# GpSimd's edge columns ahead of the difference, small steps and table sums by VectorE, two of three images in the combined form

## The chip, the cores and the metric

One Trainium2 chip, one core. The time is the device time of one execution in microseconds (us), given as the median of three runs. The engines named here are TensorE (PE: matmuls; PEld: its weight loads), VectorE (DVE), ScalarE (ACT), GpSimd (POOL) and SyncE (SP, which issues the plain transfers). SBUF is the on-chip memory, PSUM the accumulators that TensorE writes.

## What is computed

An input `x` of 160 images, 128 channels, 32x32 pixels, is group-normalised (32 groups of 4 channels, per image) and convolved with a 3x3 kernel, and the result is added to `x`. There are five sets of weights; image number `b*5+n` of the input uses set `n`. The weights are quantised in two stages from `U`, with step sizes taken from the maximum and minimum of the whole of `U`.

```python
def _L0_conv_ref(x, U):
    beta = jnp.max(U); alpha = jnp.min(U)
    s1 = (beta - alpha) / 3.0
    v1 = s1 * floor(U / s1)
    s2 = s1 / 5.0
    v2 = s2 * floor((U - v1) / s2)
    w = (v1 + v2).reshape(OUT_CH * N, IN_CH, 3, 3)
    xb = x.reshape(B // N, N * C, H, W)
    act = conv_general_dilated(xb, w, (1, 1), padding 1, feature_group_count=N)
    return act.reshape(B, C, H, W)
def _gn(v, G=32, eps=1e-5):
    g = v.reshape(B, G, C // G, H, W)
    m = mean(g, (2, 3, 4)); s = var(g, (2, 3, 4))
    return ((g - m) / sqrt(s + eps)).reshape(v.shape)
x = x + _L0_conv_ref(_gn(x), U)
```

## The kernel before

The kernel works set by set, 32 images to a set, image `i` from 0 to 159. Channels lie on the 128 partitions, an image is 1024 float32 on each. Images come in chunks of two (tile `xt`, eleven chunks in the pool), and leave by chunks too.

**Precision.** The normalised image is split into a high and a low float16 part; the weights are small multiples of one step and exact in float16.

**Two forms of an image.** Each form saves multiplications by pairing neighbours (a sum and a difference of neighbouring rows or columns, multiplied with sums and differences of taps). The loop takes one of them per image, chosen by `combined(i)` (line 563):

- *not combined* (rows): `z` is the normalised image (GpSimd, line 625, or ScalarE, line 552, for an image that starts a group of statistics), `hi` its float16 part (ScalarE, 560), `lo` the rest (VectorE, 650), and three VectorE instructions build the pair sums `rows` from `lo` (663, 671, 672). TensorE does 18 matmuls on `hi` (687) and 12 on `rows` (742): 30.
- *combined* (columns): `v` holds differences and sums of neighbouring columns of the raw image. VectorE writes most of it (602, 609), GpSimd one quarter, the difference of odd and even columns (619), and the two edge columns (590). ScalarE makes the float16 `vh` from it (637), VectorE the rest `vl` (643). TensorE does 24 matmuls (742).

`combined(i)` is true, from image 7, for odd images up to 125, for three of five up to 145 and for two of three after that: 82 images.

**The loop.** In iteration `i` TensorE runs `conv(i)` (761): first `sums_of_pairs(i+1)`, six matmuls into the bank `m2` and six into `m1`, then the main products of image `i` into its own bank pair `eo`. Beside it, each on its own engine, in program order:

- VectorE: the low part of image `i+2` (`low_combined` or `low_part` and `combinations`), one or two instructions of the next set's weights (`take(later, ...)`, fourteen instructions for each of three columns of taps), `pairs(i+1)` (799, 801: reads `m1` in PSUM and `m2`, writes `eo`), `combine(i+4)` (602, 609).
- ScalarE: the first statistics pass of an image about 14 ahead (201), the copy `sum` of the finished image `i-1` out of PSUM (827), `leave(i+1)` (790: `m2` out of PSUM), `hi` or `vh` of image `i+3`, the second statistics pass (208).
- GpSimd: the quarter of `v` or the `z` of image `i+4` (`beside_pairs`; a dependency written by hand makes it wait for the last VectorE instruction ahead of `pairs`), the transfer that adds `sum` to the image in SBUF (850, `accumulate`), the small steps of the statistics, the sums of the weight tables, and last the edge columns (590).
- SP: the store of a finished chunk (855), then the next load (426).

**The residual.** Mostly ScalarE copies the result out of PSUM and a GpSimd transfer adds it to `xt`. Where `by_hand(i)` is true (the first three images, the last four, and every eighth from image 31) VectorE adds the result to the image itself (844) and there is no transfer.

**Small steps.** The images fall into groups (2, 2, 4, 4, 4, 4, 4, then 8 each). For each group TensorE averages over channels (216, 233), ScalarE copies the results (225, 239), and GpSimd does eight small instructions (227 to 230, 243, 247, 250, 252), among them the power -0.5 (243).

**Tables.** The weights of the next set are quantised by VectorE, turned by TensorE and copied by ScalarE (496). GpSimd then makes, for each column, the sum and the difference tables (502 to 504), and after the third column the same over columns (`across`). The order of all of this is written out by hand; each engine works its own queue in order.

Of the kernel before, what the change touches and what calls it, by code (L numbers as in the profile page):

```python
# [19 lines left out]
ROW = 3  # L20
# [146 lines left out]
class Statistics:  # L167
# [5 lines left out]
    def __init__(self, nc, small, gavg, mhalf, nb, scale, name):  # L173
        self.nc, self.small, self.gavg, self.mhalf = nc, small, gavg, mhalf
        self.nb, self.scale, self.name = nb, scale, name

        self.mv = self.tile("mv", [nb, 2])
# [57 lines left out]
    def deviation(self):  # L235

        nc = self.nc
        ve = self.tile("ve", [self.nb])
        nc.scalar.activation(
            ve, self.pg[:, 1, :], ACTF.Copy, scale=1.0 / self.size, bias=EPS  # L240
        )
        self.rstd = self.tile("rstd", [self.nb])
        nc.gpsimd.tensor_tensor(self.rstd, ve, self.mhalf[:, : self.nb], ALU.pow)  # L243
# [11 lines left out]
def general_path(tc, keep, steps, x, u, out):  # L255
# [8 lines left out]
    with tc.If(far > 0), ExitStack() as ctx:  # L264
# [9 lines left out]
        for n in range(N_SETS):  # L274
# [11 lines left out]
            with tc.For_i(0, IMGS // N_SETS, 1) as b:  # L286
# [7 lines left out]
                stats.deviation()  # L294
                stats.scales()
# [22 lines left out]
class Main:  # L318
# [28 lines left out]
    FIFTHS = 126  # L347
    THIRDS = 146
    EARLY = 8
    FIRST = 3  # L350

# [5 lines left out]
    def __init__(self, tc, ctx, keep, x, u, out):  # L357
# [42 lines left out]
        self.wts, self.across = {}, {}  # L400
# [91 lines left out]
    def keep_taps(self, n, col):  # L492

        P = self.P
        wt = self.wpool.tile([P, 5, P], MM, tag=f"wt{col}", name=f"wt{n}_{col}")
        self.nc.scalar.mul(wt[:, self.G, :], self.pt, 1.0 / LIFT)  # L496
        self.wts[n, col] = wt

    def both_sums(self, total, diff, g0, g1, g2):

        pool = self.nc.gpsimd
        pool.tensor_tensor(total, g0, g2, ALU.add)
        pool.tensor_tensor(diff, total, g1, ALU.subtract)
        pool.tensor_tensor(total, total, g1, ALU.add)

    def keep_sums(self, n, col):
        wt = self.wts[n, col]
        self.both_sums(wt[:, self.SUM], wt[:, self.DIFF], *(wt[:, k] for k in range(ROW)))
        if col == self.COLS[-1]:
            across = self.wpool.tile(  # L510
                [self.P, 2, ROW, self.P], MM, tag="across", name=f"across{n}"
            )
            self.across[n] = across
            self.both_sums(
                across[:, 0], across[:, 1], *(self.wts[n, c][:, self.G] for c in range(ROW))
            )
# [69 lines left out]
    def outer_columns(self, i):  # L586

        W, H = self.W, self.H
        st, j = self.column_of(i)
        self.nc.gpsimd.tensor_scalar(  # L590
            self.view(self.v[i], 0, (512 + W // 2 - 1, 2), (W // 2, H)),
            self.view(self.image(i), 1, (W - 3, 2), (W, H)),
            st.ngm[:, j], -1.0, ALU.add, ALU.mult,
        )
# [18 lines left out]
    def beside_pairs(self, i, after):  # L613

        nc = self.nc
        if self.combined(i):
            self.v[i] = self.wide.tile([self.P, 2048], F32, tag="v", name=f"v{i}")
            even, odd = (self.image(i)[:, a::2] for a in range(2))
            ins = nc.gpsimd.tensor_sub(self.v[i][:, 1536:], odd, even)  # L619
        elif self.by_scalar_too(i):  # L620
            return
        else:
            st, j = self.column_of(i)
            z = self.z[i] = self.zpool.tile([self.P, 1024], F32, tag="z", name=f"z{i}")
            ins = nc.gpsimd.tensor_scalar(  # L625
                z, self.image(i), st.ngm[:, j], st.rstd[:, j], ALU.add, ALU.mult
            )
        self.tc.add_manual_dep(
            ins.ins, after.ins.name,
# [229 lines left out]
    def run(self):  # L859
# [75 lines left out]
        self.stats[0].deviation()  # L935
        measure(1, 2)
# [9 lines left out]
        self.stats[1].deviation()  # L946
        self.stats[1].scales()
# [38 lines left out]
        ready, middle, measured, loaded = [], [], self.EARLY, 6  # L986
        later, turned = iter(()), []
        for i in range(self.imgs):
# [15 lines left out]
            if i < self.FIRST:  # L1004
# [6 lines left out]
                if i == 0:  # L1011
                    self.stats[2].variances()
                    self.stats[2].deviation()
                    self.stats[2].scales()
# [32 lines left out]
            else:  # L1047
# [8 lines left out]
                last = take(later, i % 2, last)  # L1056
# [12 lines left out]
                for st in ready:  # L1069
                    st.deviations()  # L1070
# [8 lines left out]
            for st in middle:  # L1079
                st.deviation()  # L1080
                st.scales()
# [79 lines left out]
```

## Time and profile before

| | |
|---|---|
| median of three runs (lowest, highest) | 1014.31 us (1011.05, 1015.3) |
| the profiled execution | 1012.46 us, span 1010.8 us |
| granted TensorE clock, mean over the span | 0.992 |
| combined images / others | 82 / 78 |
| images added by a transfer / by VectorE | 137 / 23 |
| span from the `pairs` of image 64 to those of image 96 | 434.39 to 627.50 us |
| the same, image 96 to 128 | 627.50 to 820.33 us |

The profile is one execution. Its page gives busy time per engine, waits by releaser, groups of instructions with their mean durations, and shares of the sixteen transfer engines. "Busy" counts the time in which at least one instruction of the engine is open, and instructions overlap by some 0.05 to 0.1 us, so the cost of one instruction in a full queue is read from start to start in the timeline, not from its duration. The starts of line 799, one for each image, give the pace of the loop.

### The profile page before, as it was taken

The numbers are of one execution on the slowest core, as the hardware profiler recorded it, in microseconds if no ns is written. First come the engines' busy times: TensorE is split into PE (matmuls) and PEld (weight loads), VectorE is DVE, ScalarE is ACT, GpSimd is POOL, SyncE is SP. The second block draws the span as 40 slices with busy tenths as digits, with TensorE's granted clock in tenths as the row PEclk, the third lists the DMA queues.
The fourth block names the chain that finished last, engine by engine and source line by source line (L and its number), as shares of the span: only waits on it lengthen the run. The fifth ranks groups of instructions, "written<-read, shape, count | busy, mean of one in ns | idle before, by whom it ended". The sixth has DMA issues, their size and how long they took to land.

```text
span 1010.8 us, 13191 instructions
## 1 busy us (share of the span) xinstructions
PE 951.7 (94%) x4504; PEld 441.5 (44%) x4504; DVE 899.1 (89%) x1175; ACT 831.5 (82%) x1154; POOL 575.2 (57%) x622
## 2 busy tenths in 40 slices
PE   2889999998999999989999999999999989999997
PEld 1434444444444444434444444444444434444443
DVE  7988999997998999788989897988999987979995
ACT  5768989898898988889889888897988978899551
POOL 4346575665646466655556565646465776456740
PEclk9999999999999999999999999999999989999999
DMA  9528899999997988988988989998989798997774
GB/s 360 196 89 232 219 271 257 267 254 254 270 307 185 306 224 266 246 258 236 258 243 242 260 264 245 280 258 257 242 250 285 206 255 212 276 250 208 182 201 157
DMA packets 65116, 245.85 MB, mean 243 GB/s; under 512 B 5008, under 2 KB 5008, under 8 KB 65040
## 3 DMA queue, kind: packets, MB, share of 16 engines
q1 hardware_dynamic: 45312, 173.09, 48.8%
q0 software_dynamic: 19728, 71.84, 37.1%
q8 instruction: 37, 0.61, 0.2%
q14 instruction: 39, 0.32, 0.1%
HBM read 89.19 MB, written 83.89 MB: 171 GB/s over the span
## 4 chain that ended last, share of the span: by engine, by line
ACT 25%; POOL 24%; PE 18%; DVE 16%; issue 15%; DMA 1%; POOLq 0%; DVEq 0%; ACTq 0%
ACT vh L637 7%; ACT junk L208 7%; PE eo L687 6%; PE eo L742 5%; POOL v L590 4%; ACT sum L827 4%; PE m L742 3%; POOL rstd L243 3%; POOL xt L850 3%; ACT m L790 3%; POOL v L619 2%; DVE lo L650 2%; DVE v L602 2%; DVE eo L799 2%; DVE eo L801 2%
## 5 line engine op out<-in xcount | busy, mean ns | idle before, releaser
L687 PE MATMUL eo<-hi,wt 128*128 128x496 f16 (+2 forms) x1386 | 369.3, 376 | 0.8 <-ACT wt L496 0.8
L742 PEld LDWEIGHTS <-wt 128*128 128x128 f16 x1884 | 184.1, 99 | 208.4 <-issue 0.9
L637 ACT ACTIVATE vh<-v,rstd 128x2048 f16<-128x2048 f32 x82 | 164.2, 2003 | 73.9 <-POOL v L590 73.5
L643 DVE SCALAR_TENSOR_TENSOR vl<-v,rstd,vh 128x2048 f16<-128x2048 f32 x82 | 193.0, 2354 | 33.1 <-ACT vh L637 32.5
L687 PEld LDWEIGHTS <-wt 128*128 128x128 f16 x1458 | 143.1, 99 | 165.9 <-issue 2.5
L619 POOL TENSOR_TENSOR v<-xt 128x512 f32<-128x512 f32 x82 | 85.7, 1045 | 209.1 <-DVE vl L643 52.9
L742 PE MATMUL eo<-vh,wt 128*128 128x496 f16 (+1 forms) x492 | 184.3, 375 | 0.0
L742 PE MATMUL eo<-vl,wt 128*128 128x496 f16 (+1 forms) x492 | 184.2, 374 | 0.0
L201 ACT ACTIVATE junk<-xt 128x1024 f16<-128x1024 f32 x152 | 160.6, 1057 | 19.2 <-DMA xt<-in_x_dram 15.7
L208 ACT ACTIVATE junk<-xt,mv 128x1024 f16<-128x1024 f32 x152 | 174.0, 1145 | 0.1
L742 PE MATMUL eo<-rows,wt 128*128 128x496 f16 (+1 forms) x450 | 171.4, 381 | 0.0
L742 PEld LDWEIGHTS <-across 128*128 128x128 f16 x984 | 97.0, 99 | 139.6 <-issue 27.7
L827 ACT COPY sum<-eo 128x1024 f32<-128x1024 f32 x137 | 141.9, 1036 | 15.9 <-PE eo L742 15.9
L590 POOL TENSOR_SCALAR v<-xt,ngm 128x64 f32<-128x64 f32 x82 | 120.4, 1469 | 59.5 <-DVE v L602 59.2
L850 POOL DMA_DIRECT2D xt<-sum x137 | 120.8, 881 | 2.8 <-issue 1.9
L790 ACT ACTIVATE m<-m 128x512 f32<-128x512 f32 x157 | 93.7, 597 | 26.7 <-PE m L742 20.6
L742 PE MATMUL m<-vh,across 128*128 128x496 f16 (+1 forms) x246 | 93.3, 379 | 21.2 <-ACT m L790 17.1
L625 POOL TENSOR_SCALAR z<-xt,ngm,rstd 128x1024 f32<-128x1024 f32 x53 | 62.9, 1187 | 64.5 <-DVE rows L672 55.5
L602 DVE TENSOR_TENSOR v<-xt 128x960 f32<-128x960 f32 x82 | 97.4, 1187 | 0.0
L650 DVE TENSOR_TENSOR lo<-z,hi 128x1024 f16<-128x1024 f32 x78 | 96.0, 1231 | 0.0
L742 PE MATMUL m<-vl,across 128*128 128x496 f16 (+1 forms) x246 | 93.5, 380 | 0.0
L799 DVE SCALAR_TENSOR_TENSOR eo<-m1a,m 128x512 f32<-128x512 f32 x78 | 54.3, 696 | 40.7 <-ACT m L790 36.8
(131 smaller groups left out, 1301.4 us busy)
## 6 DMA issues: line engine op xcount, KB each, us to landing
xt<-in_x_dram SPq DMA_DIRECT2D x78, 1024.0 KB, 9.6
out_dram<-xt SPq DMA_DIRECT2D x78, 1024.0 KB, 5.9
xt<-sum POOLq DMA_DIRECT2D x137, 512.0 KB, 6.2
u<-in_L_conv_U_dram SPq DMA_DIRECT2D x4, 576.0 KB, 10.9
xt<-in_x_dram SPq DMA_DIRECT2D x4, 512.0 KB, 9.7
range<-in_L_conv_U_dram SPq DMA_DIRECT2D x3, 576.0 KB, 7.9
out_dram<-xt SPq DMA_DIRECT2D x3, 512.0 KB, 2.7
u<-in_L_conv_U_dram SPq DMA_DIRECT2D x2, 288.0 KB, 3.1
```

What stands on the lines that cost most here:

```text
L201: self.nc.scalar.activation(junk, image, ACTF.Copy, scale=-1.0 / image.shape[1], accum_out=self.mv[:, j, 0:1],)
L208: self.nc.scalar.activation(junk, image, ACTF.Square, bias=self.mv[:, j, 0:1], accum_out=self.mv[:, j, 1:2],)
L590: self.nc.gpsimd.tensor_scalar(self.view(self.v[i], 0, (512 + W // 2 - 1, 2), (W // 2, H)), self.view(self.image(i), 1, (W - 3, 2), (W, H) ...
L602: nc.vector.tensor_tensor(self.view(v, 1, (511, 2), (half, H), (1, half - 1)), self.view(x, 1, (1, 2), (W, H), (2, half - 1)), self.view(x ...
L637: self.nc.scalar.mul(vh, self.v[i], st.rstd[:, j])
L643: yield self.nc.vector.scalar_tensor_tensor(vl, self.v[i], st.rstd[:, j], self.hi[i], ALU.mult, ALU.subtract)
L650: self.nc.vector.tensor_sub(lo[:, 1 : self.H + 1, :].rearrange("p h w -> p (h w)"), self.z.pop(i), self.hi[i].rearrange("p h w -> p (h w)"),)
L687: nc.tensor.matmul(self.bank(target, a)[:, first:end, c0:c1], self.wts[n, col][:, k, :], tile[:, s0 : s0 + 2 * (end - first) - 1 : 2, c0 + ...
L742: self.nc.tensor.matmul(out, weights, moving, start=start and j == 0, stop=False, skip_group_check=True)
L790: self.nc.scalar.mul(m2, self.m2_ps, 0.5)
L827: nc.scalar.copy(self.as_banks(i, self.sum[i]), self.flat(i, eo))
L850: self.nc.gpsimd.dma_start(self.image(i), self.sum.pop(i), accum_op=ALU.add)
```

## The change

- `combined(i)` is `i % 3 != 1` from image 7 on: 102 images are combined, 58 are not. A group can now begin with a combined image, which needs no `z` by ScalarE.
- `by_hand(i)` holds for the first three and the last four images only.
- The edge columns (`outer_columns`) move from the end of GpSimd's work of an iteration to `beside_pairs`, ahead of the quarter of differences, and both get the dependency on the last VectorE instruction ahead of `pairs`. VectorE's `combine` of the same image comes after them.
- For all groups but those that start at images 0, 2, 4, 8 and 24 (`late`), VectorE does five small steps straight from PSUM (`deviations_by_vector`) and two more (`scales_by_vector`); GpSimd keeps the power, which runs one iteration later than before, ahead of `beside_pairs`. ScalarE no longer copies the means for them.
- The three column tables of a set are one tile. For sets 1 to 4 VectorE makes the sums: three instructions for the three columns at once and three for `across`, taken one or two at a time from `later` after the third column.
- `take(later, ...)` takes two instructions with a combined image and one otherwise (before: one with odd images, none with even ones); the instruction taken with `low_part` and the one taken where there is no `combine` stay.

```diff
@@ Statistics
         nc.scalar.activation(
             ve, self.pg[:, 1, :], ACTF.Copy, scale=1.0 / self.size, bias=EPS
         )
-        self.rstd = self.tile("rstd", [self.nb])
-        nc.gpsimd.tensor_tensor(self.rstd, ve, self.mhalf[:, : self.nb], ALU.pow)
+        self.ve = ve
+
+    def power(self):
+        self.rstd = self.tile("rstd", [self.nb])
+        return self.nc.gpsimd.tensor_tensor(
+            self.rstd, self.ve, self.mhalf[:, : self.nb], ALU.pow
+        )
+
+    def deviations_by_vector(self):
...
+        means = self.pg[:, 0, :]
+        vector.tensor_scalar_mul(self.twice, means, 2.0)
+        vector.tensor_tensor(self.dv, mv[:, :, 0], means, ALU.subtract)
+        vector.tensor_copy(self.ngm, means)
+        vector.scalar_tensor_tensor(
+            self.dv, self.dv, float(self.size), self.dv, ALU.mult, ALU.mult
+        )
+        vector.tensor_add(self.dv, self.dv, mv[:, :, 1])
+
+    def scales_by_vector(self):
...
+        vector.tensor_scalar_mul(self.rstd, self.rstd, self.scale)
+        self.shift = self.tile("shift", [self.nb])
+        vector.tensor_tensor(self.shift, self.ngm, self.rstd, ALU.mult)
@@ Main
+    HURRIED = (0, 2, 4, 8, 24)
...
+    def sums_of_set(self, n):
+        wt = self.tables[n]
+        yield from self.both_sums(
+            self.nc.vector, wt[:, :, self.SUM], wt[:, :, self.DIFF],
+            *(wt[:, :, k] for k in range(ROW)),
+        )
+        yield from self.sums_across(n, self.nc.vector)
...
+            self.stats[k].late = self.groups[k].start not in self.HURRIED
...
-        if i < self.FIFTHS:
-            return i % 2 == 1
-        return (i - self.FIFTHS) % 5 % 2 == 0 if i < self.THIRDS else i % 3 != 1
+        return i % 3 != 1
...
             self.v[i] = self.wide.tile([self.P, 2048], F32, tag="v", name=f"v{i}")
+            self.after(self.outer_columns(i), after)
             even, odd = (self.image(i)[:, a::2] for a in range(2))
             ins = nc.gpsimd.tensor_sub(self.v[i][:, 1536:], odd, even)
...
-        if i < self.FIRST or i >= self.imgs - LAST:
-            return True
-        return i > self.BY_VECTOR[-1] - 4 and i % 8 == 7
+        return i < self.FIRST or i >= self.imgs - LAST
@@ run
-                last = take(later, i % 2, last)
+                last = take(later, 2 if self.combined(i + 2) else 1, last)
+                for st in scaled:
+                    self.after(st.power(), last)
                 if i + 4 < self.imgs:
                     self.beside_pairs(i + 4, last)
...
                 for st in ready:
-                    st.deviations()
+                    if not st.late:
+                        st.deviations()
...
             for st in middle:
                 st.deviation()
-                st.scales()
+                if not st.late:
+                    st.power()
+                    st.scales()
...
-            for column in turned:
-                self.keep_column(*column)
+            for n_of, col in turned:
+                self.keep_taps(n_of, col)
+                if col == self.COLS[-1]:
+                    later = self.sums_of_set(n_of)
...
                 if self.combined(i + 4):
                     self.combine(i + 4)
-                    self.outer_columns(i + 4)
                 else:
                     take(later, 1)
                 if b == self.per_set - 4:
                     run(later)
-
-            middle, ready = ready, []
+                for st in ready:
+                    if st.late:
+                        st.deviations_by_vector()
+                for st in scaled:
+                    st.scales_by_vector()
+
+            scaled, middle, ready = [st for st in middle if st.late], ready, []
```

More of the change, by code (lines that the diff above doesn't have):

```diff
@@ L175, in __init__ @@
         self.nb, self.scale, self.name = nb, scale, name
+        self.late = False
         self.mv = self.tile("mv", [nb, 2])
@@ L241, in deviation @@
         )
+        self.ve = ve
+    def power(self):
         self.rstd = self.tile("rstd", [self.nb])
-        nc.gpsimd.tensor_tensor(self.rstd, ve, self.mhalf[:, : self.nb], ALU.pow)
+        return self.nc.gpsimd.tensor_tensor(
+            self.rstd, self.ve, self.mhalf[:, : self.nb], ALU.pow
+        )
+    def deviations_by_vector(self):
+        vector, mv = self.nc.vector, self.mv
+        self.ngm, self.twice, self.dv = (self.tile(tag, [self.nb]) for tag in ("ngm", "twice", "dv"))
+        means = self.pg[:, 0, :]
[7 more added lines that the diff above has]
+    def scales_by_vector(self):
+        vector = self.nc.vector
+        vector.tensor_scalar_mul(self.rstd, self.rstd, self.scale)
+        self.shift = self.tile("shift", [self.nb])
+        vector.tensor_tensor(self.shift, self.ngm, self.rstd, ALU.mult)
     def scales(self):
@@ L294, in general_path @@
                 stats.deviation()
+                stats.power()
                 stats.scales()
@@ L346 @@
     BY_VECTOR = (8, 10, 11, 14, 19, 24, 29, 34)
-    FIFTHS = 126
-    THIRDS = 146
     EARLY = 8
     FIRST = 3
+    HURRIED = (0, 2, 4, 8, 24)
     COLS = (1, 0, 2)
@@ L399, in __init__ @@
         self.sum = {}
-        self.wts, self.across = {}, {}
+        self.tables, self.wts, self.across = {}, {}, {}
         self.columns = []
@@ L494, in keep_taps, with both_sums, sums_across @@
         P = self.P
-        wt = self.wpool.tile([P, 5, P], MM, tag=f"wt{col}", name=f"wt{n}_{col}")
+        if n not in self.tables:
+            self.tables[n] = self.wpool.tile([P, ROW, 5, P], MM, tag="wt", name=f"wt{n}")
+        wt = self.wts[n, col] = self.tables[n][:, col]
         self.nc.scalar.mul(wt[:, self.G, :], self.pt, 1.0 / LIFT)
[L497 to L504, printed above, removed]
+    def both_sums(self, engine, total, diff, g0, g1, g2):
+        yield engine.tensor_tensor(total, g0, g2, ALU.add)
+        yield engine.tensor_tensor(diff, total, g1, ALU.subtract)
+        yield engine.tensor_tensor(total, total, g1, ALU.add)
+    def sums_across(self, n, engine):
+        across = self.across[n] = self.wpool.tile(
+            [self.P, 2, ROW, self.P], MM, tag="across", name=f"across{n}"
+        )
+        yield from self.both_sums(
+            engine, across[:, 0], across[:, 1], *(self.tables[n][:, c, self.G] for c in range(ROW))
+        )
+    def sums_of_set(self, n):
+        wt = self.tables[n]
+        yield from self.both_sums(
+            self.nc.vector, wt[:, :, self.SUM], wt[:, :, self.DIFF],
+            *(wt[:, :, k] for k in range(ROW)),
+        )
+        yield from self.sums_across(n, self.nc.vector)
     def keep_sums(self, n, col):
         wt = self.wts[n, col]
-        self.both_sums(wt[:, self.SUM], wt[:, self.DIFF], *(wt[:, k] for k in range(ROW)))
+        run(self.both_sums(
+            self.nc.gpsimd, wt[:, self.SUM], wt[:, self.DIFF], *(wt[:, k] for k in range(ROW))
+        ))
         if col == self.COLS[-1]:
[L510 to L516, printed above, removed]
+            run(self.sums_across(n, self.nc.gpsimd))
     def keep_column(self, n, col):
@@ L589, in outer_columns @@
         st, j = self.column_of(i)
-        self.nc.gpsimd.tensor_scalar(
+        return self.nc.gpsimd.tensor_scalar(
             self.view(self.v[i], 0, (512 + W // 2 - 1, 2), (W // 2, H)),
@@ L627, in beside_pairs, with after @@
             )
+        self.after(ins, after)
+    def after(self, ins, before):
         self.tc.add_manual_dep(
-            ins.ins, after.ins.name,
+            ins.ins, before.ins.name,
             mybir.DependencyInfo(mybir.DependencyClass.Sync, mybir.DependencyReason.DATA),
@@ L935, in run @@
         self.stats[0].deviation()
+        self.stats[0].power()
         measure(1, 2)
@@ L946, in run @@
         self.stats[1].deviation()
+        self.stats[1].power()
         self.stats[1].scales()
@@ L985, in run @@
         self.steps.choose()
-        ready, middle, measured, loaded = [], [], self.EARLY, 6
+        ready, middle, scaled, measured, loaded = [], [], [], self.EARLY, 6
         later, turned = iter(()), []
@@ L1013, in run @@
                     self.stats[2].deviation()
+                    self.stats[2].power()
                     self.stats[2].scales()
```

## The prediction

> **What bounds the kernel now.** I read the busy line of the page first, then busy time by stretches, the waits, the chain of waits around one stall, and VectorE's timeline.
>
> ```profile
> PE 951.7 (94%) x4504; PEld 441.5 (44%) x4504; DVE 899.1 (89%) x1175; ACT 831.5 (82%) x1154; POOL 575.2 (57%) x622
> ```
> ```profile
> 185.00:210.00 25.00, 23.49 (x114) 10.89 (x113) 22.89 (x30) 23.23 (x33) 14.04 (x14) 1.00 1.00 279
> 460.00:560.00 100.00, 98.26 (x468) 45.43 (x467) 92.24 (x123) 87.11 (x123) 59.71 (x61) 1.00 0.90 248
> ```
> After the length the columns are PE, PEld, DVE, ACT, POOL (busy), TensorE's clock, share and rate of the transfer engines. In the middle TensorE is busy 98%, and VectorE (92%) and the transfers (0.90; in one stretch 1.00) stand close behind. So a saving on TensorE is worth at most what these two have left.
>
> ```profile
> ACT vh L637 <- POOL v L590: 73.5, 42, 3.9
> DVE eo L799 <- ACT m L790: 44.1, 46, 3.6
> ```
> ```profile
> 422.57 0.38 ACT wt L496
> ...
> 425.23 1.06 POOL across L502
> ...
> 428.24 0.38 POOL v L590
> 428.62 0.02 issue
> 428.64 2.00 ACT vh L637
> ...
> 433.76 0.61 ACT m L790
> 434.36 0.04 issue
> 434.41 2.39 PE m L742 x6
> ```
> ScalarE waits 42 times for GpSimd's edge columns. At the end of a set the wait reaches TensorE: the edge columns queue behind six table sums, `vh` behind them, then ScalarE's queue up to `m`, then six matmuls (that timeline has TensorE idle 3.28 us before 434.41). In starts of line 799 (one per image) the two images from 30, 62 and 94 take 15.13, 15.14 and 15.14 us; ordinary pairs take about 12.
>
> **TensorE's saving.** Twelve matmuls of `vh` and `vl` start from 428.42 to 430.75 us: 0.212 each. A combined image is 24 of them, 5.09 us, another 30, 6.36. The new rule combines 102 images for 82: 20 x 6 x 0.212 = 25.4 us less. Small matmuls (lines 216, 233, 487) stay.
>
> **VectorE's bill**, from start to start in its timeline:
>
> ```profile
> 163.08 2.35 DVE L643 SCALAR_TENSOR_TENSOR vl<-v,rstd,vh 128x2048 f16<-128x2048 f32 x1
> 165.35 0.61 DVE L110 SCALAR_TENSOR_TENSOR tt<-nnn,s2nlo,tt 128x384 f32<-128x384 int16 x1
> ...
> 168.12 1.15 DVE L602 TENSOR_TENSOR v<-xt 128x960 f32<-128x960 f32 x1
> 169.19 0.74 DVE L609 SCALAR_TENSOR_TENSOR v<-xt,twice 128x512 f32<-128x512 f32 x1
> 169.85 1.22 DVE L650 TENSOR_TENSOR lo<-z,hi 128x1024 f16<-128x1024 f32 x1
> 171.00 0.60 DVE L111 SCALAR_TENSOR_TENSOR tt<-tt,s2r,nnn 128x384 f32<-128x384 f32 x1
> 171.53 0.68 DVE L663 TENSOR_TENSOR rows<-lo 128x1024 f16<-128x1024 f16 x1
> 172.13 0.51 DVE L671 TENSOR_TENSOR rows<-lo 128x512 f16<-128x512 f16 x1
> 172.56 0.41 DVE L672 TENSOR_TENSOR rows<-lo 128x512 f16<-128x512 f16 x1
> 172.89 0.69 DVE L799 SCALAR_TENSOR_TENSOR eo<-m1b,m 128x512 f32<-128x512 f32 x1
> 173.61 0.70 DVE L801 SCALAR_TENSOR_TENSOR eo<-m1b,m 128x512 f32<-128x512 f32 x1
> 174.22 0.55 DVE L112 TENSOR_TENSOR lt<-tt,nnn 128x384 f16<-128x384 f32 x1
> ```
> Pairs 0.72 + 0.61 = 1.33. Combined: 2.27 + 1.07 + 0.66 + 1.33 = 5.33. Not combined: 1.15 + 0.60 + 0.43 + 0.33 + 1.33 = 3.84. A quantising instruction is about 0.50 (0.53 for L111). Over the run: 20 more combined +29.8; 16 additions by hand fewer (line 844, 1.22) -19.5; 19 groups x 7 small steps (between 0.07, line 194, and 0.24, line 193; I take 0.12, as half depend on the one before) +16; 24 table sums +7 (384 float16, between 0.24 and the 0.33 of the 512 of L672; 0.30). That is +33 before what follows.
>
> **The edge columns.** Line 590 lasts 0.37 to 3.68 us, median 1.84: 1.97 on average beside VectorE's line 609, 0.38 beside `pairs`. In the new place it starts with `pairs`, so I take 0.4; the wait of `vh` for it goes, and what comes late next is VectorE's own `combine`. The new wait is line 602 for the edge columns: they end about 0.5 us after the last instruction ahead of `pairs` (line 625 started at 161.31 when that ended at 161.20; then 0.38), and `pairs` lasts 1.33, so it is hidden; without that cover 0.5 x 102. Behind it on VectorE stand the rest of `combine` and the next low part, for which TensorE waits. On GpSimd the quarter (1.03) and the adding transfer queue behind it; that transfer waits for ScalarE's `sum` anyway. The power goes ahead of both once per group: 0.82 to 3.77 us in the rows, never beside `pairs`; by the 0.82 it is hidden, by its mean of 1.82 line 602 waits 0.9 us in some 12 groups. I take nothing, the 11 us stay in the range. `rstd` and `shift` come at the end of the iteration before `vh` needs them, cover some 2.5 us (ScalarE first has `sum` and `m`); if VectorE lags, ScalarE waits with it, not TensorE first.
>
> The quarter now starts 0.5 us later and ends about 0.25 after `pairs`, in line 602. At 180.24 line 602 took 1.37 for 1.15 when the quarter ran until 180.58. So up to 0.22 for each combined image; where VectorE waits for `m` (46 of 157) nothing; I take 0.15.
>
> The Trainium skill (SBUF — State Buffer, "Who interferes with whom") says that a VectorE instruction with two SBUF inputs and a GpSimd instruction that reads SBUF exclude each other, the first to start holding the port. That agrees with 1.97 against 0.38, and speaks against this change too: the quarter, begun first, would hold line 602 for the whole overlap, 0.25 instead of 0.15, about 10 us of VectorE over the run.
>
> **Where VectorE decides.** The 42 quantising instructions of a set were spread at 3 per two images; now they come at 7 per three, within 18 images. These 18 cost VectorE 12 x 5.33 + 6 x 3.84 + 42 x 0.50 + 16 small steps x 0.12 + 12 x 0.15 = 111.7 us; TensorE 12 x 5.09 + 6 x 6.36 + 3 for small matmuls = 102.2. VectorE is 9.5 us too slow. It can run ahead: `pairs` may start some 1.9 us into an iteration and must end some 2.5 into the next, about 5 us of slack, filled in the easy stretch before. The other 14 images: TensorE 14 x 5.51 + 1.7 = 78.9, by 0.98 of the stretch above 80.5; the sums by VectorE (1.8) are hidden there. A set: 111.7 - 5 + 80.5 + 1 (VectorE never quite full) = 188.2. Before: 434.39 to 627.50 and to 820.33, 193.0 on average; gain 4.8, with sets 1 to 3 14.4. Bounds: TensorE sets the pace throughout, 102.2/0.98 + 80.5 = 184.8 (gain 24.6); no slack, 193.2 (gain 0).
>
> Set 0, images 8 to 32, took 148.1. There VectorE also has statistics by `bn_stats` (1.68 x 4): 33 x 0.50 + 6.7 + 14 x 4.83 + 3.9 - 5 = 89.7, then ten images at 5.73: 147. Gain 1 (-4 to 5). Last set: 18 images go from three in five to two in three, 18 x 0.067 x 1.27 = 1.5; gain 2 (0 to 5).
>
> **ScalarE and transfers, hidden.** ScalarE: `vh` for `hi` 20 x (1.91 - 0.94), 12 `z` fewer x 1.27, 16 `sum` more x 0.93, 18 mean copies fewer x 0.07: +18 on 831.5, with 73.5 of waiting gone. Transfers: the adding queue takes 37.1% of the span for 137, 2.74 us of all engines each; loads and stores 48.8%, 3.08 per image. Sixteen more: +43.8. A set needs 32 x 5.82 = 186.3 at most: under 188.2, barely. SP's store waits for the last adding transfer of its chunk, the load behind it, with some 3 images of lead.
>
> **The sum:** -14.4 - 1 - 2 = -17 on the span of 1010.8: 994. The median stands 3.5 above that span (1014.31): 998. What a measurement can tell from no change is about 0.5%, 5 us: below 1009 and above 1019.
>
> **Rivals.**
> *TensorE sets the pace.* If VectorE's slack takes it all: -24.6 - 5 - 3, 982. For: TensorE at 98% for long; the three stalls of 3 us go. Against: VectorE's 9.5 us.
> *No gain.* VectorE's additions, the power's 11 us and the port eat the rest: 1014. For: VectorE's busy 899 + 33 + 15 would be 96% of 985. Against: GpSimd's waits are gone.
> *Slower: the transfers.* From 110 to 930 us they are busy 750 of 820 us (shares by stretch); with 15 more adding transfers 791. That fits if they can be used above 0.965 of the time; below, ScalarE's statistics wait for loads, and all behind them. At 0.94, the best stretch of 70 us or more but one, 841: +21, 1035. For: the time per byte is work, not queueing: the last 80 us, with ten adding transfers and fifteen stores, by these rates 50 us, show a share of 0.63, 50 us. Against: 160 to 260 us ran at 0.97 with every image added, and ScalarE waited there 0.98 us for a load.
> That images are not combined as said is no rival: the rule is plain.
>
> **How the numbers follow.** Forecast 998 (own range 989 to 1008): 0.47. TensorE's pace: 0.16. No gain: 0.16, of it 0.13 within 0.5%, 0.01 faster, 0.02 slower. Transfers: 0.21, of it 0.20 slower. Faster 0.46 + 0.16 + 0.01 = 0.63, same 0.01 + 0.13 + 0.01 = 0.15, slower 0.22. The range goes from TensorE's pace with its 2% of stalls half gone (974) to short of the transfers' full price, 1024.
>
> **What would show it.** Right: 120 matmuls fewer; line 590 near 0.4; no wait of `vh` for it; no 15 us pairs at the set ends; VectorE above 95% in the quantising stretches with TensorE at some 95% there, 98% elsewhere; line 602 at 1.3. Wrong: waits of line 201 for loads with a share near 0.95 (transfers); waits of line 602 for the power; VectorE full everywhere (no gain).

## The result

The changed kernel takes 1043.72 us (median of four runs, 1042.25 to 1046.18) against 1014.8 for the kernel before in the same runs: a ratio of 1.0294 (95% interval 1.026 to 1.0328). The profiled execution has a span of 1041.6 us for 1010.8. It is slower by 29 us where 16 us less was forecast.

The busy line of the changed kernel's page, and the queue of the adding transfers (packets, MB, share of the sixteen engines):

```profile
PE 938.9 (90%) x4384; PEld 427.6 (41%) x4384; DVE 940.6 (90%) x1296; ACT 853.0 (82%) x1139; POOL 382.6 (37%) x489
```
```profile
q0 software_dynamic: 22032, 80.23, 39.8%
```

TensorE has its 120 matmuls fewer, but only 13 us less busy time; how much of the rest lies in the ends of matmuls ahead of the added waits, and how much in the granted clock (0.987 for 0.992), was not separated. VectorE has 41 us more, ScalarE 21, and GpSimd 193 less. The share of the adding queue grew from 37.1% of 1010.8 to 39.8% of 1041.6 us, 39.6 us more of all engines (forecast 43.8).

The groups of the edge columns and of VectorE's first instruction of a combined image, and the waits that matter:

```profile
L630 POOL TENSOR_SCALAR v<-xt,ngm 128x64 f32<-128x64 f32 x102 | 37.9, 372 | 332.6 <-issue 137.9 <-DVE rows L717 55.1 <-DVE vl L688 38.0
L642 DVE TENSOR_TENSOR v<-xt 128x960 f32<-128x960 f32 x102 | 136.2, 1336 | 7.2 <-POOL v L630 7.2
```
```profile
ACT junk L202 <- DMA xt<-in_x_dram: 59.1, 34, 7.8
...
DVE eo L844 <- ACT m L835: 36.9, 25, 3.6
PE m L787 <- DVE vl L688: 36.4, 24, 5.4
...
ACT vh L682 <- DVE v L649: 20.8, 19, 3.2
```

The edge columns (line 590 before, 630 now) last 0.37 us for 1.47, and ScalarE's 73.5 us of waiting for them are gone. In their place TensorE waits for VectorE's low part, ScalarE waits for VectorE's `combine`, and 34 times ScalarE waits for an image to be loaded. (Two of the 34, of 9.6 us, are at the start, as in the kernel before, where all such waits came to 15.7.)

Busy time by stretches tells more. In each pair of lines the first is a stretch in which the next set's weights are quantised, the second one without (columns as before: length, PE, PEld, DVE, ACT, POOL, clock, share and rate of the transfers):

```profile
270.00:380.00 110.00, 98.06 (x460) 43.77 (x459) 105.87 (x151) 94.86 (x127) 38.64 (x47) 1.00 0.94 255
385.00:450.00 65.00, 61.62 (x292) 27.87 (x291) 58.08 (x77) 59.09 (x79) 25.79 (x31) 1.00 0.99 264
470.00:580.00 110.00, 99.41 (x462) 44.50 (x461) 105.87 (x149) 93.78 (x125) 39.48 (x47) 0.98 0.92 249
585.00:650.00 65.00, 61.58 (x284) 28.03 (x283) 57.74 (x73) 59.19 (x79) 25.63 (x30) 0.97 0.99 267
```

With quantising VectorE is busy 96% and TensorE 89 to 90%; without it VectorE falls to 89%, and the transfers stand at 0.99. No engine is full over the whole run, but in each stretch one engine, or the transfers, is within a few per cent of full.

How VectorE holds TensorE is seen in the timelines of the changed kernel around 340 us, VectorE's, one line of TensorE's, and GpSimd's:

```profile
336.32 0.69 DVE L844 SCALAR_TENSOR_TENSOR eo<-m1b,m 128x512 f32<-128x512 f32 x1
337.04 0.70 DVE L846 SCALAR_TENSOR_TENSOR eo<-m1b,m 128x512 f32<-128x512 f32 x1
338.63 1.98 DVE L642 TENSOR_TENSOR v<-xt 128x960 f32<-128x960 f32 x1 [0.89 <-POOL v L630]
340.54 0.74 DVE L649 SCALAR_TENSOR_TENSOR v<-xt,twice 128x512 f32<-128x512 f32 x1
341.20 0.22 DVE L268 TENSOR_SCALAR rstd<-rstd,lift 128x8 f32<-128x8 f32 x1
341.45 0.17 DVE L270 TENSOR_TENSOR shift<-ngm,rstd 128x8 f32<-128x8 f32 x1
341.54 2.34 DVE L688 SCALAR_TENSOR_TENSOR vl<-v,rstd,vh 128x2048 f16<-128x2048 f32 x1
```
```profile
343.93 0.38 PE L787 MATMUL m<-vl,across 128*128 128x512 f16 x1 [3.21 <-DVE vl L688]
```
```profile
336.55 1.67 POOL L247 TENSOR_TENSOR rstd<-ve,mhalf 128x8 f32<-128x8 f32 x1 [4.47 <-ACT junk L209]
338.22 0.37 POOL L630 TENSOR_SCALAR v<-xt,ngm 128x64 f32<-128x64 f32 x1
338.56 1.03 POOL L660 TENSOR_TENSOR v<-xt 128x512 f32<-128x512 f32 x1
```

Here VectorE runs without a gap but one: its line 642 waits 0.89 us for the edge columns, which stood behind the power (line 247), and then lasts 1.98 us beside the quarter of differences (line 660). TensorE has the high part of an image and waits 3.21 us for the low one.

### The profile page after: what moved, and what is told of

The parts are those of the page before. It is cut to its first block, busy times and chain, and to the rows that moved or that the text cites. A ratio compares the mean times of both kernels' runs of the same rounds, so it can differ in the third digit from the quotient of the medians.

```text
span 1041.6 us, 13067 instructions
## 1 busy us (share of the span) xinstructions
PE 938.9 (90%) x4384; PEld 427.6 (41%) x4384; DVE 940.6 (90%) x1296; ACT 853.0 (82%) x1139; POOL 382.6 (37%) x489
## 3 DMA queue, kind: packets, MB, share of 16 engines
q0 software_dynamic: 22032, 80.23, 39.8%
## 4 chain that ended last, share of the span: by engine, by line
DVE 45%; DMA 18%; issue 15%; PE 10%; POOL 7%; ACT 4%; SPq 0%; POOLq 0%; ACTq 0%; DVEq 0%
DVE vl L688 11%; DVE v L642 7%; DMA xt<-in_x_dram 7%; DMA xt<-sum 7%; DVE eo L844 5%; DMA u<-in_L_conv_U_dram 4%; PE eo L787 4%; DVE v L649 4%; DVE lo L695 3%; DVE eo L846 3%; PE eo L732 2%; POOL rstd L247 2%; PE m L787 2%; DVE tt L110 1%; POOL v L660 1%
## 5 line engine op out<-in xcount | busy, mean ns | idle before, releaser
L732 PE MATMUL eo<-hi,wt 128*128 128x496 f16 (+3 forms) x1026 | 273.5, 377 | 2.6 <-DVE eo L846 1.6
L688 DVE SCALAR_TENSOR_TENSOR vl<-v,rstd,vh 128x2048 f16<-128x2048 f32 x102 | 239.2, 2345 | 3.0 <-ACT vh L682 2.7
L787 PE MATMUL eo<-vh,wt 128*128 128x496 f16 (+1 forms) x612 | 230.7, 377 | 4.1 <-DVE eo L846 3.8
L787 PE MATMUL eo<-vl,wt 128*128 128x496 f16 (+1 forms) x612 | 230.6, 377 | 0.0
L682 ACT ACTIVATE vh<-v,rstd 128x2048 f16<-128x2048 f32 x102 | 203.9, 1999 | 31.1 <-DVE v L649 20.8
L787 PEld LDWEIGHTS <-across 128*128 128x128 f16 x1224 | 121.4, 99 | 200.4 <-issue 70.3
L870 ACT COPY sum<-eo 128x1024 f32<-128x1024 f32 x153 | 160.8, 1051 | 40.2 <-PE eo L787 39.8
L630 POOL TENSOR_SCALAR v<-xt,ngm 128x64 f32<-128x64 f32 x102 | 37.9, 372 | 332.6 <-issue 137.9
L642 DVE TENSOR_TENSOR v<-xt 128x960 f32<-128x960 f32 x102 | 136.2, 1336 | 7.2 <-POOL v L630 7.2
L787 PE MATMUL eo<-rows,wt 128*128 128x512 f16 x330 | 126.0, 382 | 0.0
L844 DVE SCALAR_TENSOR_TENSOR eo<-m1b,m 128x512 f32<-128x512 f32 x79 | 54.9, 695 | 34.9 <-ACT m L835 26.6
L649 DVE SCALAR_TENSOR_TENSOR v<-xt,twice 128x512 f32<-128x512 f32 x102 | 75.7, 742 | 4.3 <-POOL twice L279 4.3
```

The lines of the kernel that those rows point to most:

```text
L642: nc.vector.tensor_tensor(self.view(v, 1, (511, 2), (half, H), (1, half - 1)), self.view(x, 1, (1, 2), (W, H), (2, half - 1)), self.view(x ...
L649: nc.vector.scalar_tensor_tensor(v[:, 1024:1536], even, st.twice[:, j], odd, ALU.add, ALU.add)
L682: self.nc.scalar.mul(vh, self.v[i], st.rstd[:, j])
L688: yield self.nc.vector.scalar_tensor_tensor(vl, self.v[i], st.rstd[:, j], self.hi[i], ALU.mult, ALU.subtract)
L732: nc.tensor.matmul(self.bank(target, a)[:, first:end, c0:c1], self.wts[n, col][:, k, :], tile[:, s0 : s0 + 2 * (end - first) - 1 : 2, c0 + ...
L787: self.nc.tensor.matmul(out, weights, moving, start=start and j == 0, stop=False, skip_group_check=True)
```

## The experiments

Each ratio is to the kernel before, run on the same chip, with its 95% interval. The starts of VectorE's `pairs` (one for each image) give the time of a stretch of images; those in this table are read from the timelines of the profiled executions, in us. Gains and losses in us in the text are differences of medians; the medians of the kernel before lay between 1014.8 and 1019.2 us beside the several runs, so such a difference can be off by some 4 us, and where that matters the ratios are given too.

| images | before | changed | edge columns alone | changed, no quantising | changed, no adding transfers | changed, neither |
|---|---|---|---|---|---|---|
| 8 to 24 | 97.5 | 111.7 | 95.1 | 98.5 | 111.5 | 98.4 |
| 34 to 52 (quantising) | 105.9 | 117.4 | 103.9 | 107.4 | 113.5 | 101.0 |
| 52 to 64 | 76.2 | 70.1 | 68.9 | 70.6 | 67.1 | 66.4 |
| 66 to 84 (quantising) | 107.1 | 117.7 | 104.5 | 107.0 | 115.2 | 100.5 |
| 84 to 96 | 74.9 | 70.3 | 69.0 | 69.8 | 66.7 | 67.2 |
| 32 to 64, the whole set | 192.7 | 198.5 | 185.2 | 189.6 | 191.8 | 178.7 |

### Parts undone in the changed kernel, and one part alone

**Quantising spread wider.**

```diff
-                last = take(later, 2 if self.combined(i + 2) else 1, last)
+                last = take(later, 1, last)
...
-                if b == self.per_set - 4:
+                if b in (self.per_set - 4, self.per_set - 2):
                     run(later)
```

> The changed kernel with the quantising instructions of the next set spread wider: five per three images instead of seven, so that they fill some 25 images of a set and not 18 (the sums of the tables are finished two images before the set ends). No work is added or removed. My theory: VectorE sets the pace of the stretch with quantising (6.4 us per image in the trace of the changed kernel) and the transfers that of the rest (5.8, share 0.98), and neither can lend time to the other; spreading evens them out: 25 images x (4.83 + 0.84 + 0.20) + 4 for the wait for the weights + 7 x 5.8 = 191.5 to 193 per set for 198.9, in all about 1020 us. Rival 1, the transfers alone hold the whole loop: no change, 1041 to 1046. Rival 2, VectorE's sum of work over the whole loop: no change either, 1041 to 1046. Rival 3, the new waits (power, edge columns, port): no change.

Measured: 1029.28 us, ratio 1.0105 (1.0051 to 1.0159). All three rivals had no change; the same work in another order gives back 14 us, so the order counts. The size is short of the 24 that I expected (by the ratios 19 us came back): the stretch still takes 6.0 to 6.3 us per image.

**Additions by VectorE again.**

```diff
-        return i < self.FIRST or i >= self.imgs - LAST
+        if i < self.FIRST or i >= self.imgs - LAST:
+            return True
+        return i > self.BY_VECTOR[-1] - 4 and i % 8 == 7
```

> The changed kernel with every eighth image from 31 on added by VectorE again, as in the kernel before; 16 adding transfers fewer, 16 copies by ScalarE fewer. My theory: the stretch with quantising loses 2 to 3 us per set to the 1.22 us additions, the stretch without them wins about 2 as the share of the transfers falls by some 6%; 1040 to 1046, no change that counts. Rival 1, the transfers alone: 16 x 2.74 = 44 us of them go, about 1010. Rival 2, VectorE's sum of work: +20 us, about 1062.

Measured: 1033.85 us, ratio 1.0132 (1.0097 to 1.0166). I had expected no change, and 10 us came back (16 by the ratios). So the transfers held more than I thought, though far from the 44 us of rival 1; VectorE's sum of work, which had 1062, falls.

**The old density.**

```diff
-        return i % 3 != 1
+        if i < 126:
+            return i % 2 == 1
+        return (i - 126) % 5 % 2 == 0 if i < 146 else i % 3 != 1
```

> The changed kernel with the old rule for which images are combined (odd ones up to 125, three of five up to 145, then two of three): 20 images fewer, TensorE +25 us, VectorE -31 us; all else as changed. My theory: per set the stretch with quantising falls by 6.6 us (9 x 5.33 + 9 x 3.84 for 12 and 6 of them), the other rises by 2.4 as TensorE sets its pace: -4.2 x 3, -5 in the first set, about 1023. Rival 1, the transfers alone: no change, 1041. Rival 2, VectorE's sum of work: -31, about 1012. Rival 4, TensorE has become the bound: +25, about 1068.

Measured: 1006.03 us, ratio 0.9871 (0.984 to 0.9902). The rule on which the forecast's gain of 25 us rested costs 38 us here. That is more than my theory had and beyond rival 2 too. What is left then is seen in one stretch of this run, with the transfers at 1.02 of their time:

```profile
360.00:460.00 100.00, 98.30 (x469) 45.72 (x468) 85.45 (x119) 89.31 (x126) 37.32 (x44) 1.00 1.02 276
```

**The edge columns alone**, in the kernel before:

```diff
             self.v[i] = self.wide.tile([self.P, 2048], F32, tag="v", name=f"v{i}")
+            self.after(self.outer_columns(i), after)
             even, odd = (self.image(i)[:, a::2] for a in range(2))
...
                     self.combine(i + 4)
-                    self.outer_columns(i + 4)
```

> The kernel before with one part of the change alone: the edge columns ahead of the difference, both held until the last VectorE instruction ahead of the pairs. Expected: line 590 falls from a mean of 1.47 to about 0.4 us, the 73.5 us in which ScalarE waits for it go, TensorE's stalls at the ends of the sets shrink; 1003 to 1010 us. Rival 3, the new place costs VectorE more (line 602 longer by 0.15 us and more, waiting for GpSimd) than the wait was worth: 1015 or above.

Measured: 984.27 us, ratio 0.9646 (0.9615 to 0.9678), the fastest of all versions that compute the whole. One part alone wins twice the gain that I forecast for all parts. Its busy line, a stretch, and the group of the edge columns:

```profile
PE 945.1 (96%) x4504; PEld 441.4 (45%) x4504; DVE 903.2 (92%) x1175; ACT 833.0 (85%) x1154; POOL 497.8 (51%) x622
```
```profile
260.00:360.00 100.00, 99.83 (x479) 46.92 (x480) 94.62 (x126) 90.83 (x128) 52.11 (x64) 1.00 0.95 265
```
```profile
L590 POOL TENSOR_SCALAR v<-xt,ngm 128x64 f32<-128x64 f32 x82 | 31.9, 389 | 216.6 <-DVE vl L648 44.7 <-DVE rows L677 35.8 <-DVE tt L109 25.0
```

TensorE is full, at 5.79 us per image, and VectorE and the transfers have 5% left. The other parts of the change, but for the small steps, spend those 5%.

### The other parts, one at a time on top of the edge columns

**No additions by VectorE** (the diff of "Additions by VectorE again" the other way round, on top of the edge columns).

> The kernel before with the edge columns moved (984 us alone, TensorE 100% busy in the middle) and, as a second part of the change, no image added by VectorE in the middle. VectorE -20 us, ScalarE +15, the adding transfers +44 us of all engines. If the transfers count: a set needs 32 x 5.82 = 186 us of them, the version with all parts but the density took 189.5 at a share of 0.97 to 1.02; +3 to 4 per set and some in the first, 994 to 1000 us. Rival, VectorE is what is short: 984 or a little less.

Measured: 1001.04 us, ratio 0.9856 (0.9836 to 0.9875): 17 us more than with the edge columns alone (21 by the ratios), a little above what the transfers' price had, though VectorE has 20 us less to do. A stretch of it, transfers at 0.99:

```profile
260.00:360.00 100.00, 97.78 (x462) 45.36 (x461) 90.33 (x119) 89.49 (x126) 52.56 (x66) 0.98 0.99 274
```

**Small steps and table sums by VectorE** (the changed kernel with the old density, additions by VectorE, `take(later, i % 2, last)`, and a second `run(later)` two images before a set ends).

> The kernel before with the edge columns moved and, as a second part, the small steps of the late groups and the table sums of sets 1 to 4 by VectorE (two more points at which a set's last instructions are taken, so that the sums are ready; density, additions by VectorE and rate of quantising as before). VectorE +23 us, spread over the run: it goes from 94 to 97% and TensorE still sets the pace; the stall at set ends (189.5 for 185.2 us in set 3, 13 us for two images) goes. 978 to 986 us. Rival 3, the small steps cost by their new waits (the power one iteration later, in front of the edge columns; rstd late for vh): 995 or more.

Measured: 986.09 us, ratio 0.9701 (0.9678 to 0.9724): 2 us more by the medians, 5 to 6 by the ratios, whose intervals just touch: small, if anything. Where TensorE sets the pace these steps are nearly hidden. The stall at the end of set 3 stayed: TensorE waits there 4.3 us for VectorE's `across`, where with the edge columns alone it waits 2.3 us for GpSimd's, so the engine that makes the sums is not its cause.

**Two of three images combined.**

```diff
-        if i < self.FIFTHS:
-            return i % 2 == 1
-        return (i - self.FIFTHS) % 5 % 2 == 0 if i < self.THIRDS else i % 3 != 1
+        return i % 3 != 1
...
-                last = take(later, i % 2, last)
+                last = take(later, 1, last)
```

> The kernel before with the edge columns moved and, as a second part, two of three images combined from image 7 on (and quantising at five per three images, so that it ends in time; additions by VectorE, small steps and sums as before). TensorE -25 us, VectorE +30. My theory: VectorE becomes the bound, 25 images x (4.83 + 0.84 + 0.15 + 0.15) + 7 x 5.6 = 188 to 190 per set for 186.6: 988 to 1000. Rival, TensorE still paces: 984 - 25 = 960 to 965.

Measured: 1014.71 us, ratio 0.9979 (0.9966 to 0.9991): 30 us more, where I had expected 4 to 16 and the rival some 20 less. VectorE at 98% and TensorE below 97%, in the stretch where the version with the edge columns alone had 95 and 100:

```profile
260.00:360.00 100.00, 96.50 (x460) 44.57 (x459) 98.02 (x118) 92.35 (x126) 48.53 (x61) 1.00 0.93 261
```

**Quantising earlier**: `take(later, 2 if self.combined(i + 2) else 1, last)` for `take(later, i % 2, last)`.

> The kernel before with the edge columns moved and, as a second part, the quantising instructions taken earlier, four per two images for three (two with each combined image). No work added. VectorE needs 21 images x (4.59 + 1.0 + 0.25) = 122.6 where TensorE needs 21 x 5.79 = 121.6: 984 to 992. If VectorE could run ahead of TensorE by an image, as I had put it, nothing at all would be seen: 982 to 986.

Measured: 996.64 us, ratio 0.9808 (0.9791 to 0.9824): 12 us more with no work added. The stretches with quantising take 107.0, 107.4 and 107.3 us (103.9, 104.5 and 104.5 with the edge columns alone). Those without take 69.3 and 69.4 for 68.9 and 69.0; nothing could come back there, as TensorE paced them before (only the stall at the end of set 3 shrinks, 70.0 for 73.3 from image 116 to 128). What TensorE waits for in sets 1 to 3 (241 to 810 us) is one thing alone:

```profile
PE small L233 <- POOL dv L230: 7.9, 8, 1.5
```

That is not VectorE but a small step of GpSimd's, whose `z` and quarter, ahead in its queue, are tied by hand to VectorE's last instruction ahead of `pairs`. Only in images 8 to 32 does TensorE wait for VectorE, 4.6 us. So this run shows that earlier quantising costs time, but it is no clean test of how far VectorE may fall behind.

The four prices on top of 984 are 17, 2, 30 and 12 us: 1045 in all, for 1043.7 measured with all parts. That this fits is in part luck: in ratios the sum is 1.041 for 1.029, the third price includes a wider quantising, and the rate of the changed kernel, seven per three images, was run only in the changed kernel and its variants.

### What holds each stretch: work taken out of the changed kernel

**Without quantising** (`if n + 1 < N_SETS:` becomes `if False:`, and all sets read `self.wts[0, ...]` and `self.across[0]`).

> The changed kernel without the quantising of sets 1 to 4 and their tables: all sets use the weights of set 0, so images 32 to 159 are convolved with the wrong weights. VectorE -84 us (4 x 21) and -7 for table sums, their four loads of weights gone. My theory: the stretches at 6.4 us per image fall to the pace of the transfers, 32 x 5.8 = 186 per set for 198.6, the first set by some 10: about 990 us. Rival 1, the transfers alone: 1035 or more. Rival 5, TensorE's own pace: 182 per set, 970 to 975.

**Without the adding transfers** (`accumulate` only drops the tile).

> The changed kernel without the adding transfers: the result of the convolution is not added to the images, the output is x for 153 of them. 153 x 2.74 us of all transfer engines and GpSimd's issues go. My theory: the stretches with quantising stay at 6.3 to 6.4 us per image (VectorE), the others fall from 5.8 to 5.6: 1041 - 3 x 3 - 6 (no more waits for the weights) = about 1025 us. Rival 1, the transfers alone hold the loop: 970 to 980.

**Without either.**

> The changed kernel without either: no quantising of sets 1 to 4 and no adding transfers. My theory: TensorE's pace is left, 5.64 us per image at 0.98 to 1.0, 181 to 184 per set: 962 to 975 us. Rival 3, the new waits of the changed order hold it (power, edge columns, rstd late): 990 or more.

Measured: 1000.08 us (ratio 0.9823, 0.9777 to 0.9868), 1016.61 (1.0001, 0.998 to 1.0022) and 958.98 (0.9417, 0.9371 to 0.9462). In the same order a stretch of each, for the first two the one with quantising in the changed kernel:

```profile
270.00:380.00 110.00, 105.39 (x499) 48.81 (x498) 95.84 (x115) 102.14 (x138) 44.65 (x54) 1.00 1.00 270
```
```profile
270.00:375.00 105.00, 98.15 (x458) 44.43 (x457) 103.09 (x147) 93.56 (x124) 23.21 (x28) 0.98 0.54 171
```
```profile
260.00:360.00 100.00, 99.53 (x475) 46.50 (x474) 90.52 (x112) 96.83 (x131) 26.45 (x32) 1.00 0.60 190
```

Without quantising the transfers are full (1.00) and hold the loop at 5.9 to 6.0 us per image in every set. They do it through ScalarE, which waits 37 times for an image to be loaded, and TensorE then for its `m`; without the adding transfers only the two waits at the start are left. The waits without quantising, ScalarE's and TensorE's, and ScalarE's without the adding transfers:

```profile
ACT junk L202 <- DMA xt<-in_x_dram: 69.9, 37, 8.1
```
```profile
PE m L787 <- ACT m L835: 22.3, 16, 3.2
```
```profile
ACT junk L202 <- DMA xt<-in_x_dram: 9.9, 2, 8.1
```

Without the transfers VectorE is full (98%) where it quantises, 6.3 to 6.4 us per image, and the rest runs at TensorE's 5.6. Without either TensorE is full, at 5.58. So neither saving alone frees the kernel: 44 and 27 us, together 85. The two expectations were off by 8 to 10 us, in opposite directions, and the third by 3.

How far VectorE falls behind can be read without the adding transfers. The first lines are TensorE's: the first matmuls of the pair sums of images 34 and 40, and its first long wait for VectorE. The others are VectorE's `pairs` of the same two images:

```profile
260.11 0.81 PE L787 MATMUL m<-rows,wt 128*128 128x512 f16 x3
...
293.80 0.82 PE L787 MATMUL m<-rows,wt 128*128 128x512 f16 x3
...
299.80 0.38 PE L787 MATMUL m<-vl,across 128*128 128x512 f16 x1 [1.21 <-DVE vl L688]
```
```profile
263.18 0.70 DVE L844 SCALAR_TENSOR_TENSOR eo<-m1a,m 128x512 f32<-128x512 f32 x1
...
300.52 0.69 DVE L844 SCALAR_TENSOR_TENSOR eo<-m1a,m 128x512 f32<-128x512 f32 x1
```

`pairs` starts 3.07 us after those matmuls at image 34 and 6.72 at image 40. Up to image 39 TensorE does not wait for VectorE; from there on it does. In the whole of set 1 (247.39 to 440.31 us) its waits are these:

```profile
PE m L787 <- DVE vl L688: 7.5, 5, 3.1
PE eo L787 <- DVE eo L846: 0.8, 2, 0.4
PE small L234 <- DVE dv L263: 0.5, 1, 0.5
```

That is 8.8 us, 2.5 of it after image 52, while VectorE catches up; sets 2 and 3 have 10.8 and 10.7. Without either, TensorE waits 0.5 us for VectorE in set 1 and 0.9 in set 2.

### Two terms of the sum, and two tries for a faster version

**The quarter as a fill**: `nc.gpsimd.memset(self.v[i][:, 1536:], 0.0)` for `tensor_sub`.

> The changed kernel with GpSimd's quarter (the difference of odd and even columns) replaced by a fill with zeros of the same tile, which writes the same place and reads nothing; the convolution of the combined images is wrong by that quarter. If the port is what makes line 642 last 1.34 us (1.19 for the same instruction in the kernel before), it falls to 1.15 to 1.2, and of that 0.15 to 0.2 the 18 images of the stretch with quantising get 12 x 0.2 = 2.4 us per set back: 1043 - 4 x 2.4 = about 1033 us. If the quarter's run into line 602 cost nothing: 1041 to 1046.

Measured: 1030.11 us, ratio 1.0156 (1.01 to 1.0213), 14 us less than the changed kernel; the group of line 642 is below the 1.19 us of the kernel before:

```profile
L642 DVE TENSOR_TENSOR v<-xt 128x960 f32<-128x960 f32 x102 | 117.5, 1152 | 8.3 <-POOL v L630 8.3
```

The fill differs in two ways: it reads nothing, and it lasts 0.51 us where the difference lasts 1.03. Of the 102 lines 642 of the changed kernel 28 don't overlap the difference and last 1.15 us; 63 overlap it by 0.28 us on average and last 1.31; 11, where the power went ahead, overlap it by 0.96 and last 1.98. Of those of the run with the fill 90 begin after it has ended; 12 overlap it, by 0.41 on average, and last 1.16. So beside a difference line 642 is longer by nearly the overlap, and beside a fill it is not.

**The weights earlier**: `load_set(n + 2)` at `b == 28`, in place of `load_set(n + 1)` at `b == 0`.

> The changed kernel with the weights of the set after the next loaded four images before a set ends, once the quantising has read the last ones, so that they are there when quantising begins. VectorE waited for them 3.98, 2.13 and 0.52 us in sets 1 to 3. If such a wait falls in the stretch that VectorE paces, all of it comes back, 1037 us or so; if the transfers are as full at the new place as at the old, it moves into ScalarE's waits for images, 1041 to 1046.

Measured: 1042.29 us, ratio 1.0261 (1.0207 to 1.0315), no change. The stretch 34 to 52 wins 1.9 us and 32 to 34 loses 2.3: where the transfers are full, an earlier load only moves the wait.

**Four of seven combined** on top of the edge columns (`i % 7 % 2 == 0` up to 125, then two of three; `take(later, int(i % 3 > 0), last)`).

> The kernel before with the edge columns moved (984 us), four of seven images combined up to 125 and two of three after that, quantising slightly earlier (two of three iterations take one more). TensorE there is 100% busy at 5.79 us per image and VectorE 94.5%. TensorE -0.09 us per image, VectorE +0.11 and more of the port: 975 to 982 if VectorE's 5% can be used up; 985 to 992 if, as the other runs have it, VectorE can't be filled beyond 97%.

**Two of three only from image 126 on**, on top of the edge columns.

> The kernel before with the edge columns moved (984 us) and two of three images combined only from image 126 on, where nothing is quantised (before: three of five up to 145). The run with two of three throughout took 101.4 us from image 128 to 146 where the one with the edge columns alone took 103.8: 980 to 983. If the saving needs more room on VectorE than is there: 984 to 986.

Measured: 993.39 us (ratio 0.9763, 0.9718 to 0.9809) and 986.72 (0.9722, 0.9673 to 0.9771). Neither beats the edge columns alone. The first falls short of its 975 to 982; the second does what it should from image 128 to 146 (101.3 us for 103.8), but no gain shows in the whole.

## Why the prediction was wrong

- **What bounds the kernel.** Right that TensorE bounds it, that VectorE and the transfers stand close behind, and that a saving on TensorE is worth at most what those two have left. I then didn't hold to it: with the waits for GpSimd gone, they had 5% left, and the parts of the change ask for more of each.
- **TensorE's saving.** 120 matmuls fewer, as counted; worth nothing here. With the edge columns moved the extra density costs 30 us. It shows only where nothing else is full: 178.5 us per set without quantising and adding transfers, for 185.2 with the edge columns alone.
- **VectorE's bill.** Its rows were right: 18 images with quantising were put at 111.7 us of VectorE, and in the changed kernel it is busy 111.3 from image 34 to 52. They take 113.5 to 115.2 without the adding transfers, and 117.4, 117.7 and 114.3 with them.
- **The step that failed** is the one after it: "It can run ahead: `pairs` may start some 1.9 us into an iteration and must end some 2.5 into the next, about 5 us of slack, filled in the easy stretch before." By it TensorE was to wait for VectorE some 3.4 us per set (188.2 against 184.8). It waits 14.2, 11.8 and 10.7 us in sets 1 to 3 of the changed kernel, and 8.8, 10.8 and 10.7 without the adding transfers. Some slack is there: VectorE fell 3.65 us further behind before TensorE waited. But it was spent within five of the 18 images, and 2.5 us of it came back as waits while VectorE caught up, so that about 1 us of the 5 was left in that set. In set 1 of the changed kernel the wait of 3.98 us for the weights, at image 34, took the slack at once. ScalarE is not what holds VectorE in that stretch: without the adding transfers VectorE waits there 0.8 us for the edge columns, 0.2 for TensorE and for nothing else.
- **The other 14 images** were put at 80.5 by TensorE's pace. They take 81 to 84, and 78 without the adding transfers, which is 14 times TensorE's 5.58; so the transfers set their pace, and TensorE's is 5.58, not 5.75. That the transfers need 186.3 us per set against 188.2 I took for room ("barely"); it is no room if the time is spent in a stretch where another engine is full. That the eleven chunks can't carry loads over from one stretch to the other is my reading; only one earlier load was tried.
- **The sum per set** came to 188.2 and measured 198.5, 199.6 and 198.6, 10.7 more on average. Without the adding transfers the sets take 191.8, 193.0 and 191.7: 6.7 of the 10.7 go with them, among them the waits for the weights (3.98, 2.13 and 0.52 us), and 4.0 stay. Those 4.0 are 6.4 more in the 18 images, where neither the slack nor the power came as summed, less 2.4 in the other 14. Such shares don't add up: without quantising 8.8 us per set go, without either 20.4. The first set (147 forecast, 157.1 measured) failed mostly by VectorE: 155.5 without the adding transfers, 142.5 without quantising. Images 128 on gained nothing (179.2 for 178.3).
- **The edge columns.** Line 590 (now 630) at 0.4 us, the wait of `vh` gone: right. Its worth was not set out at all; it was mixed into the pace of TensorE. Alone it is 31 to 35 us, all of the gain there is.
- **The port.** 0.15 us were taken for each combined image. Line 642 lasts 1.336 us on average against 1.187 before, but undisturbed it lasts 1.15: the collision costs 0.18 on average, 0.15 in the ordinary case and 0.83 behind the power. By the rule that the prediction cites it estimated 0.25, the whole overlap; measured is 0.13 us less than the overlap, in both cases. The run with the fill, which is also the shorter instruction, has the two together at 14 us of time, since part of it falls where VectorE is full. The Trainium skill (SBUF — State Buffer, "Who interferes with whom") says that a VectorE instruction with two SBUF inputs does not contend with a GpSimd instruction that only writes: the 12 overlapping fills, with line 642 at 1.16, bear that out.
- **Rivals.** "Slower: the transfers" had the right sign and half of the mechanism; its test was wrong, since the transfers can be used at 0.99 to 1.02 and still hold a stretch. "TensorE sets the pace" (982) is what the edge columns alone reach. "No gain" named VectorE for the whole run; it is full in part of it.
- **The power** ahead of the edge columns was taken at nothing. Line 642 waits 7.2 us for the edge columns in the changed kernel, and in the 11 images where the quarter then runs through it, it lasts 9.1 us longer in all: 16 us of VectorE. Where TensorE sets the pace most of this is hidden (the run with the small steps); where VectorE is full it is not: from the `pairs` of image 45 to those of 46 it takes 8.34 us, where from 42 to 43 it takes 6.35; of the 2.0 us more, 0.34 are the two small steps.

## What to carry to other kernels

When several engines are between 90 and 98% busy, do the sum for each stretch with its own full engine, and count the slack between two engines only once: it is spent in a few iterations and has to be caught up afterwards; averages over a loop hide two bounds that take turns. A change of many parts is best taken one part at a time: here one part won 3.5%, and the rest spent that and 3% more. Count a resource as free only if it is free in the stretch in which the change asks for it.

## What the runs showed of the hardware that I had not expected

A GpSimd instruction on 64 columns takes 0.37 to 0.39 us on average beside VectorE's `pairs`, which read PSUM, where it took 1.97 beside its line 609. The same holds the other way round: VectorE's line 642 lasts 1.15 us alone, 1.31 with 0.28 us of a GpSimd difference beside its start, 1.98 with 0.96, and 1.16 beside a fill. The transfer engines can be busy 0.99 to 1.02 of the time over 100 us without a loss in rate (270 to 276 GB/s, for 248 at a share of 0.90); in the runs with every image added they then hold the loop at 5.8 to 6.0 us per image.
